# Reordering the setup of a four-layer graph-attention kernel: mask rows, first loads, and which step's work goes first

## The chip, the cores and the metric

The kernel runs on one NeuronCore of one Trainium2 chip. The metric is the device time of one execution in microseconds (us), the median of several executions. Before the change it is 2712.34 us (three runs, 2709.53 to 2713.56).

Six instruction streams appear in the profile: PE (TensorE matmul) with its weight loads PEld, DVE (VectorE), ACT (ScalarE), POOL (GpSimd) and SP (SyncE). A name with a q (ACTq, SPq) is the instruction queue of that engine; a DMA is issued there, and while an issue waits or is still being written out, nothing behind it in that queue starts.

## The reference, cut to what matters

Sixteen graphs of 1024 nodes with 256 features share one 1024 x 1024 integer adjacency matrix. Four attention layers follow one another:

```python
h = jnp.maximum(_layernorm(x, axis=-1), 0.0)
x = x + _L0_gnn_ref(h, adj, L0_gnn_W, L0_gnn_a)      # layers 1, 2, 3 likewise
# one layer, H heads of D features (H = 4, 1, 4, 1)
q = (h @ W).reshape(B, N, H, D)
e = e_src[:, :, None, :] + e_dst[:, None, :, :]      # q . a_src and q . a_dst, an N x N matrix per head
e = jnp.where(e >= 0, e, ALPHA * e)
e = jnp.where(mask, e, NEG_INF)                      # adj > 0 in layers 0 and 1, adj != 0 in 2 and 3
attn = jax.nn.softmax(e, axis=2)
out = elu(attn @ q)                                  # relu in layer 3
```

## The kernel before

A *step* is one layer of one graph; there are 64, and four graphs are in flight. For each step the kernel makes layer-norm statistics (`bn`), normalised rows (`xn`), their transposes (`hT`), projections (`whx`, `sd`) and a row `grow` that goes out to DRAM and comes back broadcast to all partitions (`gs`, copied into PSUM as `g`). Then, for each head, DVE makes eight tiles `w` (weights times mask) and PE multiplies them with `whx`. The masks are made once, from `adj`, transposed by PE. P = 128, C = 8, HALF = 4, K = 2.

```python
    def mask_block(jc):                       # one of 8 column blocks of adj
        def fetch_block():
            st["raw"] = work.tile([P, C, P], I32, name="w", bufs=WBUFS)
            nc.scalar.dma_start(out=st["raw"], in_=adj.rearrange("(c p) j -> p c j", p=P)[
                :, :, jc * P:(jc + 1) * P])                                       # L155
        def sign():
            nc.vector.tensor_scalar(st["sgn"][:, 0], st["raw"], -1.0, 1.0, ...)   # L160
        def turn():
            pm = st["pm"] = ps_acc.tile([P, C, P], BF16, name="acc")
            for c in range(C):
                nc.tensor.transpose(pm[:, c, :], st["sgn"][:, 0, c, :], identb)   # L166
        def mask():
            nc.vector.tensor_scalar(masks[0][:, jc, :], pm, 0.0, None, op0=ALU.is_gt)  # L170
            nc.scalar.activation(masks[1][:, jc, :], pm, AF.Square)                    # L171

    # preparation(n), 20 pieces: stats(0), stats(1), normalise(0), normalise(1),
    #   then per half: transpose k = 0, 1 (L221, L222) and four project(c) (L233 to L244),
    #   then factors (L251 to L255), rows (L260 to L264), fetch_heads (L278)
    #   stats:     8 bn_stats on DVE (L191), then 10 small POOL operations (L198 to L207)
    #   normalise: 4 ACT operations (L213)
    # weight_columns(l): vectors (DMA of a, L114), columns (8 DVE operations and sq, L124 to L131),
    #   bound (PE L137, DVE top L140, four POOL operations L141 to L144)
    # broadcast: g <- gs on ACT (L284);  weights: w on DVE (L289);  aggregate: PE L305, ACT L309
    ...
        load(0)                               # x of graph 0, SP queue (L177)
        load_weights(0)                       # SP queue (L103)
        layer[0][0]()                         # the vectors a of layer 0, SP queue
        for jc in range(C):
            blocks[jc][0]()                   # eight loads of adj, ACT queue
        load(1)
        ...                                   # preparation of step 0, mixed with the masks
        done["prepared"] = 1
        plan(1)
        planned = 2
        prepare(-2)                           # step 1: statistics to the first four projections
        emit_tiles(C, must=True)              # step 0: first two g, first eight w
        prepare(-1)                           # step 1: the rest
        for i in range(1, STREAMS):
            load_weights(i)
            if i > 1:
                load(i)
        for l, at in ((1, 1), (2, 8 * 3 + 5), (3, 8 * 5 + 5)):
            for i, piece in enumerate(layer[l]):
                later[at + i] = piece         # run after group `at + i`, eight groups a step
```

Of the kernel before, what the change touches and what calls it, by code (L numbers as in the profile page):

```python
# [23 lines left out]
F32 = mybir.dt.float32  # L24
BF16 = mybir.dt.bfloat16
I32 = mybir.dt.int32
U8 = mybir.dt.uint8
AF = mybir.ActivationFunctionType
ALU = mybir.AluOpType
# [3 lines left out]
P = 128  # L33
EPS = 1e-5
SHIFT = 60.0
STREAMS = 4
WBUFS = 18
# [20 lines left out]
def kernel(ctx: ExitStack, tc: tile.TileContext, x, adj, ws, avs, out):  # L58
    nc = tc.nc
    B, N, F = x.shape  # L60
    C = N // P
    K = F // P
    HALF = C // 2

    const = ctx.enter_context(tc.tile_pool(name="const", bufs=1))
# [3 lines left out]
    neghalf = const.tile([P, C], F32, name="neghalf")  # L69
    nc.gpsimd.memset(neghalf, -0.5)  # L70
    half1 = const.tile([P, 1], F32, name="half1")
# [3 lines left out]
    identb = const.tile([P, P], BF16, name="identb")  # L75

    masks = [const.tile([P, C, N], U8, name=f"mask{i}") for i in range(2)]
    wx = []
# [5 lines left out]
    cbias = [const.tile([P, 1], F32, name=f"cbias{l}") for l in range(len(LAYERS))]  # L84
    shift60 = const.tile([P, 1], F32, name="shift60")
    nc.gpsimd.memset(shift60, SHIFT)

    xpool = ctx.enter_context(tc.tile_pool(name="xpool", bufs=STREAMS))
    prep = ctx.enter_context(tc.tile_pool(name="prep", bufs=2))
    small = ctx.enter_context(tc.tile_pool(name="small", bufs=4))  # L90
    work = ctx.enter_context(tc.tile_pool(name="work", bufs=2))
# [7 lines left out]
    xs = {}  # L99
    state = [dict() for _ in steps]  # L100

    def load_weights(l):
        nc.sync.dma_start(out=wx[l][:, :, 0:F], in_=ws[l].rearrange("(k p) f -> p k f", p=P))  # L103

    def weight_columns(l):

        H, slope, hs, _ = LAYERS[l]
        D = F // H
        st = {}

        def vectors():
            st["a"] = prep.tile([P, HALF, H, D], F32, name="e")
            for part in range(2):
                nc.sync.dma_start(  # L114
                    out=st["a"][:, part],
                    in_=bass.AP(tensor=avs[l].tensor, offset=avs[l].offset + part * D,
                                ap=[[0, P], [hs, H], [1, D]]),
                )

        def columns():  # L120
            for k in range(K):
                for part in range(2):
                    prod = st["a"][:, 2 + part]
                    nc.vector.tensor_mul(  # L124
                        prod, wx[l][:, k, 0:F].rearrange("p (h d) -> p h d", h=H),
                        st["a"][:, part])
                    nc.vector.tensor_reduce(
                        wx[l][:, k, F + part * H:F + (part + 1) * H], prod, AX.X, ALU.add)
            st["sq"] = small.tile([P, K, H], F32, name="sq", bufs=1)
            wd = wx[l][:, :, F + H:F + 2 * H]  # L130
            nc.vector.tensor_tensor(st["sq"], wd, wd, op=ALU.mult)  # L131

        def bound():

            pn = ps_p.tile([P, H], F32, name="pp")
            for k in range(K):
                nc.tensor.matmul(pn, lhsT=ones, rhs=st["sq"][:, k, :], start=(k == 0),  # L137
                                 stop=(k == K - 1))
            top = small.tile([P, 1], F32, name="top", bufs=1)
            nc.vector.tensor_reduce(top, pn, AX.X, ALU.max)  # L140
            nc.gpsimd.tensor_tensor(top, top, half1, op=ALU.pow)  # L141
            nc.gpsimd.tensor_scalar(cbias[l], top, 16.01, None, op0=ALU.mult)
            nc.gpsimd.tensor_scalar(nbias[l], top, -16.01 * slope, None, op0=ALU.mult)
            nc.gpsimd.tensor_scalar(rbias[l], top, -16.01 * (1.0 - slope), SHIFT,  # L144
                                    op0=ALU.mult, op1=ALU.add)

        return vectors, columns, bound

    def mask_block(jc):

        st = {}

        def fetch_block():
            st["raw"] = work.tile([P, C, P], I32, name="w", bufs=WBUFS)
            nc.scalar.dma_start(out=st["raw"], in_=adj.rearrange("(c p) j -> p c j", p=P)[  # L155
                :, :, jc * P:(jc + 1) * P])

        def sign():
            st["sgn"] = work.tile([P, 2, C, P], BF16, name="w", bufs=WBUFS)
            nc.vector.tensor_scalar(st["sgn"][:, 0], st["raw"], -1.0, 1.0, op0=ALU.max,  # L160
                                    op1=ALU.min)

        def turn():
            pm = st["pm"] = ps_acc.tile([P, C, P], BF16, name="acc")
            for c in range(C):
                nc.tensor.transpose(pm[:, c, :], st["sgn"][:, 0, c, :], identb)  # L166

        def mask():
            pm = st["pm"].rearrange("p c i -> p (c i)")
            nc.vector.tensor_scalar(masks[0][:, jc, :], pm, 0.0, None, op0=ALU.is_gt)  # L170
            nc.scalar.activation(masks[1][:, jc, :], pm, AF.Square)  # L171

        return fetch_block, sign, turn, mask

    def load(b):
        xs[b] = xpool.tile([P, C, F], F32, name="x")
        nc.sync.dma_start(out=xs[b], in_=x[b].rearrange("(c p) f -> p c f", p=P))  # L177

    def preparation(n):

        b, l = steps[n]
# [4 lines left out]
        def stats(half):  # L186
            if half == 0:
                st["bn"] = small.tile([P, C, 6], F32, name="bn")
            bn = st["bn"]
            for c in range(half * HALF, (half + 1) * HALF):  # L190
                nc.vector.bn_stats(bn[:, c, :], xs[b][:, c, :])  # L191
            if half == 1:

                m0, s0, m1, s1 = (bn[:, :, i] for i in (1, 2, 4, 5))
                rstd = st["rstd"] = small.tile([P, C], F32, name="rstd")
                shift = st["shift"] = small.tile([P, C], F32, name="shift")
                dev = small.tile([P, C], F32, name="dev")
                nc.gpsimd.tensor_tensor(dev, m0, m1, op=ALU.subtract)  # L198
                nc.gpsimd.tensor_tensor(dev, dev, dev, op=ALU.mult)
                nc.gpsimd.tensor_scalar(dev, dev, 0.25, EPS, op0=ALU.mult, op1=ALU.add)  # L200
                nc.gpsimd.tensor_tensor(rstd, s0, s1, op=ALU.add)
                nc.gpsimd.tensor_scalar(rstd, rstd, 1.0 / F, None, op0=ALU.mult)
                nc.gpsimd.tensor_tensor(rstd, rstd, dev, op=ALU.add)
                nc.gpsimd.tensor_tensor(rstd, rstd, neghalf, op=ALU.pow)  # L204
                nc.gpsimd.tensor_tensor(shift, m0, m1, op=ALU.add)
                nc.gpsimd.tensor_tensor(shift, shift, rstd, op=ALU.mult)
                nc.gpsimd.tensor_scalar(shift, shift, -0.5, None, op0=ALU.mult)  # L207

        def normalise(half):
            xn = st["xn", half] = prep.tile([P, HALF, F], F32, name="xn")  # L210
# [165 lines left out]
    def prepare(upto):  # L376

        while agenda and agenda[0][0] <= upto:
            _, n, piece, last = agenda.pop(0)
            piece()  # L380
            if last:
                done["prepared"] = n + 1
# [53 lines left out]
    ending = []  # L436
    later = {}
    with tc.manual_schedule():
        blocks = [mask_block(jc) for jc in range(C)]
        layer = [weight_columns(l) for l in range(L)]  # L440
        load(0)
        load_weights(0)
        layer[0][0]()
        for jc in range(C):
            blocks[jc][0]()
        load(1)
        nc.vector.tensor_copy(identb, ident)
        first = [piece for _, piece in preparation(0)]
        first[0]()
        first[1]()  # L450
        layer[0][1]()
        layer[0][2]()
        first[2]()
        first[3]()
        for jc in range(3):
            for piece in blocks[jc][1:]:
                piece()

        for i, jc in ((4, 3), (6, 4), (10, 5), (12, None), (14, None)):
            if jc is not None:  # L460
                blocks[jc][1]()
            first[i]()
            first[i + 1]()
            if i == 6:
                first[8]()
                first[9]()
            if jc is not None:
                blocks[jc][2]()
                blocks[jc][3]()
        for piece in first[16:]:  # L470
            piece()
        for jc in range(6, C):
            for piece in blocks[jc][1:]:
                piece()
        done["prepared"] = 1
        plan(1)
        planned = 2
        prepare(-2)
        emit_tiles(C, must=True)
        prepare(-1)  # L480
        for i in range(1, STREAMS):
            load_weights(i)
            if i > 1:
                load(i)

        for l, at in ((1, 1), (2, 8 * 3 + 5), (3, 8 * 5 + 5)):
            for i, piece in enumerate(layer[l]):
                later[at + i] = piece
        for n in range(len(steps)):
            for k, (h, i0, per) in enumerate(groups(n)):  # L490
# [52 lines left out]
```

## Time and profile before

| | |
|---|---|
| span of the profiled execution | 2711.9 us |
| PE busy | 2567.2 us, 95% |
| DVE busy | 1900.3 us, 70% |
| ACT busy | 1229.6 us, 45% |
| POOL busy | 992.3 us, 37% |
| PE busy in the first 121 us | 58.22 us |
| first `w` tile on DVE | 78.25 us after the start |
| transfers, mean of the span | 48 GB/s |

The span is one program on one core, so a wait anywhere shows up in the time only if PE, or whatever PE waits for, is held by it. Three views are used. The chain of waits goes back from the last instruction, at each step to what released it. The timeline has start, duration, engine, line, operation, output and input, the count of merged instructions, and in square brackets the idle time ahead and what ended it. The table by stages gives the busy time of every engine in a stretch.

### The profile page before, as it was taken

The page shows a single profiled execution, that of the slowest core. Times are in us where ns is not written, and L with a number is a line of the kernel's source. Part 1 is how long each engine was busy: PE and PEld are TensorE (multiplying, and loading weights), DVE is VectorE, ACT ScalarE, POOL GpSimd, SP SyncE. Part 2 cuts the span into 40 slices and gives each one's busy share as a digit, 9 for nine tenths or more (in the row PEclk, how much of TensorE's full clock was granted, in tenths as well). Part 3 has the DMA queues.
Part 4 walks back from the last instruction along what each step waited for, and adds up shares of the span by engine and source line. Part 5 has one row for each costly group of instructions (what it writes and reads, how often), then busy time and mean ns, then how long its engine had stood idle before and what let it go on. Part 6 is the DMA issues. An engine that isn't in the chain of part 4 may idle for free.

```text
span 2711.9 us, 89498 instructions
## 1 busy us (share of the span) xinstructions
PE 2567.2 (95%) x40080; PEld 2269.2 (84%) x40080; DVE 1900.3 (70%) x2041; ACT 1229.6 (45%) x3337; POOL 992.3 (37%) x1242
## 2 busy tenths in 40 slices
PE   3799999999999999999999999999999999999998
PEld 2688888888888888888888888888888888788876
DVE  3796686477875688666876778748687567678752
ACT  3344445444354554544444454544435444444431
POOL 2133424423424534344242353442332443443321
PEclk9899999999999999999999999999999999999999
DMA  3211011012122011002201211101212110011111
GB/s 117 87 42 45 10 45 41 19 62 66 41 72 71 27 49 41 18 33 72 73 33 49 72 33 42 41 25 57 67 39 72 59 45 18 33 41 42 33 33 55
DMA packets 70846, 130.12 MB, mean 48 GB/s; under 512 B 6208, under 2 KB 49984, under 8 KB 70464
## 3 DMA queue, kind: packets, MB, share of 16 engines
q1 hardware_dynamic: 62144, 120.21, 13.5%
q8 instruction: 316, 5.18, 0.8%
q10 hardware_dynamic: 8320, 4.19, 0.6%
q14 instruction: 66, 0.54, 0.1%
HBM read 106.95 MB, written 17.43 MB: 46 GB/s over the span
## 4 chain that ended last, share of the span: by engine, by line
PE 81%; DVE 8%; ACT 4%; issue 3%; POOL 2%; DMA 1%; ACTq 0%; DVEq 0%; SPq 0%; POOLq 0%
PE acc L305 61%; PE pp L233 16%; DVE w L289 6%; PE pp L221 4%; ACT xn L213 1%; DVE bn L191 1%; DMA w<-in_adj 1%; ACT whx L235 1%; ACT g L284 1%; POOL rstd L204 0%; ACT e L339 0%; POOL y L330 0%; ACT whx L239 0%; PE pp L260 0%; DMA x<-in_x 0%
## 5 line engine op out<-in xcount | busy, mean ns | idle before, releaser
L305 PE MATMUL acc<-whx,w 128*64 128x65 f32 x36864 | 1951.0, 242 | 42.0 <-DVE w L289 28.6
L305 PEld LDWEIGHTS acc<-whx,w 128*64 128x64 f32 x36864 | 1766.8, 145 | 225.2 <-issue 70.4
L289 DVE SCALAR_TENSOR_TENSOR w<-g,rcol,mask 128x1024 f32<-128x1024 f32 x1280 | 1544.1, 1273 | 458.3 <-ACT g L284 412.3
L309 ACT ACTIVATE y<-acc 128x260 f32<-128x260 f32 (+1 forms) x512 | 196.8, 384 | 1085.8 <-PE acc L305 1085.0
L233 PE MATMUL pp<-wx,hT 128*128 128x258 f32 (+1 forms) x2048 | 513.2, 394 | 9.0 <-ACT hT L222 7.6
L330 POOL TENSOR_TENSOR y<-y,r 128x1024 f32<-128x1024 f32 x128 | 242.5, 1899 | 594.9 <-DVE r L326 594.9
L233 PEld LDWEIGHTS pp<-wx,hT 128*128 128x128 f32 x2048 | 375.1, 191 | 79.6 <-ACT hT L222 9.9
L346 POOL TENSOR_TENSOR x<-x,e 128x1024 f32<-128x1024 f32 x96 | 226.7, 2366 | 278.0 <-DVE e L345 264.2
L244 POOL TENSOR_TENSOR whx<-whx 128x256 f32<-128x256 f32 x256 | 159.9, 630 | 444.9 <-ACT whx L242 443.5
L213 ACT ACTIVATE xn<-x,shift,rstd 128x256 f32<-128x256 f32 x512 | 264.1, 590 | 126.3 <-POOL shift L207 126.0
L345 DVE SCALAR_TENSOR_TENSOR e<-e,y 128x1024 f32<-128x1024 f32 x96 | 117.6, 1225 | 197.0 <-ACT e L339 197.0
L235 ACT ACTIVATE whx<-pp,nbias 128x4 f32<-128x4 f32 (+1 forms) x512 | 135.0, 264 | 163.1 <-PE pp L233 151.8
L221 PE MATMUL pp<-ident,xn 128*128 128x128 f32 x1024 | 158.0, 287 | 39.0 <-ACT xn L213 28.3
L191 DVE BATCH_NORM_STATS2 bn<-x 128x6 f32<-128x256 f32 x512 | 172.9, 407 | 16.9 <-DMA x<-in_x 14.2
L221 PEld LDWEIGHTS pp<-ident,xn 128*128 128x128 f32 x1024 | 117.3, 144 | 76.7 <-ACT xn L213 36.3
L284 ACT ACTIVATE g<-gs 128x1024 f32<-128x1024 f32 x160 | 162.3, 1018 | 5.3 <-DVE w L289 5.3
L222 ACT ACTIVATE hT<-pp 128x512 f32<-128x512 f32 x256 | 143.2, 592 | 18.5 <-PE pp L221 16.5
L198 POOL TENSOR_TENSOR dev<-bn 128x8 f32<-128x8 f32 x64 | 16.4, 256 | 290.7 <-DVE bn L191 290.7
L239 ACT ACTIVATE whx<-pp,whx 128x256 f32<-128x256 f32 x256 | 121.7, 475 | 0.0
L339 ACT ACTIVATE e<-e 128x1024 f32<-128x1024 f32 x96 | 100.8, 1050 | 33.1 <-POOL e L335 33.1
L204 POOL TENSOR_TENSOR rstd<-rstd,neghalf 128x8 f32<-128x8 f32 x64 | 106.7, 1668 | 5.0
L335 POOL TENSOR_SCALAR e<-y 128x1024 f32<-128x1024 f32 x96 | 100.0, 1042 | 8.5
(45 smaller groups left out, 553.8 us busy)
## 6 DMA issues: line engine op xcount, KB each, us to landing
gs<-grow SPq DMA_DIRECT2D x160, 512.0 KB
x<-in_x SPq DMA_DIRECT2D x16, 1024.0 KB
out<-x SPq DMA_DIRECT2D x32, 512.0 KB
w<-in_adj ACTq DMA_DIRECT2D x8, 512.0 KB
wx<-in_L_gnn_W SPq DMA_DIRECT2D x4, 256.0 KB
e<-in_L_gnn_a SPq DMA_DIRECT2D x8, 128.0 KB
grow<-gT SPq DMA_DIRECT2D x32, 16.0 KB
grow<-gT SPq DMA_DIRECT2D x32, 4.0 KB
```

Of the source, the lines that this page charges most:

```text
L191: nc.vector.bn_stats(bn[:, c, :], xs[b][:, c, :])
L213: nc.scalar.activation(xn[:, q, :], xs[b][:, c, :], AF.Identity, bias=st["shift"][:, c:c + 1], scale=st["rstd"][:, c:c + 1])
L221: nc.tensor.transpose(pt[:, q, :], st["xn", half][:, q, k * P:(k + 1) * P], ident)
L233: nc.tensor.matmul(pw, lhsT=st["hT", half][:, k, q * P:(q + 1) * P], rhs=wx[l][:, k, :], start=(k == 0), stop=(k == K - 1))
L235: nc.scalar.activation(whx[:, c, :, D], pw[:, F + H:F + 2 * H], AF.Exp, bias=nbias[l], scale=slope)
L244: nc.gpsimd.tensor_tensor(whx[:, c, :, 0:D], whx[:, c, :, 0:D], whx[:, c, :, D:D + 1].to_broadcast([P, H, D]), op=ALU.mult)
L284: nc.scalar.activation(g, state[n]["gs", h], AF.Copy)
L289: nc.vector.scalar_tensor_tensor(w, state[n]["g", h], state[n]["rcol"][:, jc, h:h + 1], masks[LAYERS[steps[n][1]][3]][:, jc, :], op0=ALU.m ...
L305: nc.tensor.matmul(acc[o % P:o % P + cols, q, :], lhsT=st["w", h, jc][:, o:o + cols], rhs=st["whx"][:, jc, h, :], start=(jc == 0), stop=(j ...
L309: nc.scalar.activation(st["y"][:, i0:i0 + per, h, :], acc, AF.Copy)
L330: nc.gpsimd.tensor_tensor(yh, yh, r[:, :, None].to_broadcast([P, HALF * H, D]), op=ALU.mult)
L346: nc.gpsimd.tensor_add(xh, xh, e)
```

## The change

It rearranges the setup, so that the first step's work is held up by less, and leaves the steps' arithmetic as it is. The mask matrices come out the same.

1. `adj` is loaded in eight row chunks, each a contiguous row of 4 KB per partition, on the SP queue behind x of graph 0; before, it was eight column blocks in pieces of 512 B on the ACT queue. Each chunk is transposed into a column strip of the masks.
2. x of graph 0 comes in two loads, and step 0's statistics are combined for each half on DVE (all but the power) instead of once on POOL. A one-element `Exp` on ACT stands ahead of the first real one.
3. The transposed chunks 0 to 3 lie in the PSUM buffers of `g`, two to a buffer, so the second mask (`Square` on ACT) can be made from them after step 0's row is out.
4. Step 0's first `g` and `w` stand ahead of step 1's preparation (all but its statistics) in the order of instructions.
5. The weights of layer 1 are loaded early; `columns` and `bound` of layers 1 to 3 move to other groups.

```diff
-    def load_weights(l):
-        nc.sync.dma_start(out=wx[l][:, :, 0:F], ...)
+    def load_weights(l, queue=nc.sync):
+        queue.dma_start(out=wx[l][:, :, 0:F], ...)
...
-    def mask_block(jc):
+    pairs = {}
+    def mask_rows(c):
-            nc.scalar.dma_start(out=st["raw"], in_=adj.rearrange("(c p) j -> p c j", p=P)[
-                :, :, jc * P:(jc + 1) * P])
+            st["raw"] = work.tile([P, N], I32, name="w", bufs=WBUFS)
+            nc.sync.dma_start(out=st["raw"], in_=adj[c * P:(c + 1) * P, :])
...
         def turn():
-            pm = st["pm"] = ps_acc.tile([P, C, P], BF16, name="acc")
+            if c < HALF:
+                if c % 2 == 0:
+                    pairs[c // 2] = ps_g.tile([P, 2, C, P], BF16, name="g")
+                pm = pairs[c // 2][:, c % 2]
+            else:
+                pm = ps_acc.tile([P, C, P], BF16, name="acc")
...
-        def mask():
+        def positive():
+            nc.vector.tensor_scalar(masks[0][:, :, c * P:(c + 1) * P], st["pm"], 0.0, None,
+                                    op0=ALU.is_gt)
+        def nonzero():
+            nc.scalar.activation(masks[1][:, :, c * P:(c + 1) * P], st["pm"], AF.Square)
...
-            if half == 1:
-                ...                            # ten operations of 128 x 8 on POOL
+            if n == 0:
+                combine(slice(half * HALF, (half + 1) * HALF), nc.vector)
+            elif half == 1:
+                combine(slice(0, C), nc.gpsimd)    # the power is on POOL in both
...
-        load(0)
-        load_weights(0)
-        layer[0][0]()
-        for jc in range(C):
-            blocks[jc][0]()
+        load(0, 2)
+        layer[0][0](nc.scalar)
+        load_weights(0, nc.scalar)
+        for c in range(C):
+            blocks[c][0]()
         load(1)
+        load_weights(1)
+        nc.scalar.activation(warm, half1, AF.Exp)
...
+        # order of the second mask's chunks: 0, 4, 5, 6, 1, 2, 3, 7
+        first[0](); first[1](); first[2]()         # step 0: both halves' statistics, normalise(0)
+        layer[0][1]()                              # columns
+        first[3]()
+        sign_and_mask(False)                       # sign and turn of chunk 0
+        layer[0][2]()                              # bound
+        sign_and_mask()                            # sign and turn of the next, first mask of the last
+        for at in (4, 10):                         # one half each
+            first[at](); first[at + 1]()           # transposes
+            sign_and_mask()
+            first[at + 2](); first[at + 3]()       # two projections
+            sign_and_mask()
+            other_mask(1)
+            first[at + 4](); first[at + 5]()
+            sign_and_mask()
+            other_mask(1)
+        for piece in first[16:]:                   # row out, fetch
+            piece()
+        sign_and_mask()
+        other_mask(C)
...
-        prepare(-2)
+        for _ in range(2):                         # step 1: its statistics alone
+            agenda.pop(0)[2]()
         emit_tiles(C, must=True)
         prepare(-1)
-        for i in range(1, STREAMS):
+        for i in range(2, STREAMS):
             load_weights(i)
-            if i > 1:
-                load(i)
-        for l, at in ((1, 1), (2, 8 * 3 + 5), (3, 8 * 5 + 5)):
-            for i, piece in enumerate(layer[l]):
+            load(i)
+        for l, at in ((1, 1), (2, 8 * 3 + 3), (3, 8 * 5 + 3)):
+            for i, piece in zip((0, 1, 7), layer[l]):
                 later[at + i] = piece
```

More of the change, by code (lines that the diff above doesn't have):

```diff
@@ L86 @@
     nc.gpsimd.memset(shift60, SHIFT)
+    warm = const.tile([P, 1], F32, name="warm")
     xpool = ctx.enter_context(tc.tile_pool(name="xpool", bufs=STREAMS))
@@ L100 @@
     state = [dict() for _ in steps]
-    def load_weights(l):
-        nc.sync.dma_start(out=wx[l][:, :, 0:F], in_=ws[l].rearrange("(k p) f -> p k f", p=P))
+    def load_weights(l, queue=nc.sync):
+        queue.dma_start(out=wx[l][:, :, 0:F], in_=ws[l].rearrange("(k p) f -> p k f", p=P))
     def weight_columns(l):
@@ L109, in weight_columns, with vectors @@
         st = {}
-        def vectors():
+        def vectors(queue=nc.sync):
             st["a"] = prep.tile([P, HALF, H, D], F32, name="e")
             for part in range(2):
-                nc.sync.dma_start(
+                queue.dma_start(
                     out=st["a"][:, part],
@@ L147, in weight_columns, with fetch_rows @@
         return vectors, columns, bound
-    def mask_block(jc):
+    pairs = {}
+    def mask_rows(c):
         st = {}
-        def fetch_block():
-            st["raw"] = work.tile([P, C, P], I32, name="w", bufs=WBUFS)
-            nc.scalar.dma_start(out=st["raw"], in_=adj.rearrange("(c p) j -> p c j", p=P)[
-                :, :, jc * P:(jc + 1) * P])
+        def fetch_rows():
+            st["raw"] = work.tile([P, N], I32, name="w", bufs=WBUFS)
+            nc.sync.dma_start(out=st["raw"], in_=adj[c * P:(c + 1) * P, :])
         def sign():
-            st["sgn"] = work.tile([P, 2, C, P], BF16, name="w", bufs=WBUFS)
+            st["sgn"] = work.tile([P, 2, N], BF16, name="w", bufs=WBUFS)
             nc.vector.tensor_scalar(st["sgn"][:, 0], st["raw"], -1.0, 1.0, op0=ALU.max,
@@ L163, in turn, with load @@
         def turn():
-            pm = st["pm"] = ps_acc.tile([P, C, P], BF16, name="acc")
-            for c in range(C):
-                nc.tensor.transpose(pm[:, c, :], st["sgn"][:, 0, c, :], identb)
-        def mask():
[L169 to L175, printed above, removed]
+            if c < HALF:
[4 more added lines that the diff above has]
+                pm = ps_acc.tile([P, C, P], BF16, name="acc")
+            st["pm"] = pm
+            for jc in range(C):
+                nc.tensor.transpose(pm[:, jc, :], st["sgn"][:, 0, jc * P:(jc + 1) * P], identb)
+        def positive():
[3 more added lines that the diff above has]
+            nc.scalar.activation(masks[1][:, :, c * P:(c + 1) * P], st["pm"], AF.Square)
+        return fetch_rows, sign, turn, positive, nonzero
+    def load(b, parts=1):
         xs[b] = xpool.tile([P, C, F], F32, name="x")
-        nc.sync.dma_start(out=xs[b], in_=x[b].rearrange("(c p) f -> p c f", p=P))
+        xb = x[b].rearrange("(c p) f -> p c f", p=P)
+        for i in range(parts):
+            q = slice(i * C // parts, (i + 1) * C // parts)
+            nc.sync.dma_start(out=xs[b][:, q], in_=xb[:, q])
     def preparation(n):
@@ L191, in stats @@
                 nc.vector.bn_stats(bn[:, c, :], xs[b][:, c, :])
-            if half == 1:
[L194 to L207, printed above, removed]
+            if n == 0:
+                combine(slice(half * HALF, (half + 1) * HALF), nc.vector)
+            elif half == 1:
+                combine(slice(0, C), nc.gpsimd)
@@ new lines, in combine @@
+        def combine(q, engine):
+            bn = st["bn"]
+            m0, s0, m1, s1 = (bn[:, q, i] for i in (1, 2, 4, 5))
+            if q.start == 0:
+                st["rstd"] = small.tile([P, C], F32, name="rstd")
+                st["shift"] = small.tile([P, C], F32, name="shift")
+                st["dev"] = small.tile([P, C], F32, name="dev")
+            rstd, shift, dev = (st[i][:, q] for i in ("rstd", "shift", "dev"))
+            engine.tensor_tensor(dev, m0, m1, op=ALU.subtract)
+            engine.tensor_tensor(dev, dev, dev, op=ALU.mult)
+            engine.tensor_scalar(dev, dev, 0.25, EPS, op0=ALU.mult, op1=ALU.add)
+            engine.tensor_tensor(rstd, s0, s1, op=ALU.add)
+            engine.tensor_scalar(rstd, rstd, 1.0 / F, None, op0=ALU.mult)
+            engine.tensor_tensor(rstd, rstd, dev, op=ALU.add)
+            nc.gpsimd.tensor_tensor(rstd, rstd, neghalf[:, q], op=ALU.pow)
+            engine.tensor_tensor(shift, m0, m1, op=ALU.add)
+            engine.tensor_tensor(shift, shift, rstd, op=ALU.mult)
+            engine.tensor_scalar(shift, shift, -0.5, None, op0=ALU.mult)
@@ L438 @@
     with tc.manual_schedule():
-        blocks = [mask_block(jc) for jc in range(C)]
+        blocks = [mask_rows(c) for c in range(C)]
         layer = [weight_columns(l) for l in range(L)]
-        load(0)
-        load_weights(0)
-        layer[0][0]()
-        for jc in range(C):
-            blocks[jc][0]()
+        load(0, 2)
[3 more added lines that the diff above has]
+            blocks[c][0]()
         load(1)
+        load_weights(1)
@@ L447, with sign_and_mask @@
+        nc.scalar.activation(warm, half1, AF.Exp)
         nc.vector.tensor_copy(identb, ident)
         first = [piece for _, piece in preparation(0)]
+        turned, signed, masked = iter(range(C)), iter(range(C)), iter((0, 4, 5, 6, 1, 2, 3, 7))
+        def sign_and_mask(second=True):
+            c = next(signed, None)
+            if c is not None:
+                blocks[c][1]()
+                blocks[c][2]()
+            if second:
+                c = next(turned, None)
+                if c is not None:
+                    blocks[c][3]()
@@ L449, with other_mask @@
+        def other_mask(count):
+            for _ in range(count):
+                c = next(masked, None)
+                if c is not None:
+                    blocks[c][4]()
         first[0]()
         first[1]()
+        first[2]()
         layer[0][1]()
+        first[3]()
+        sign_and_mask(False)
         layer[0][2]()
[L453 to L469, printed above, removed]
+        sign_and_mask()
@@ L470 @@
+        for at in (4, 10):
+            first[at]()
+            first[at + 1]()
+            sign_and_mask()
+            first[at + 2]()
+            first[at + 3]()
+            sign_and_mask()
+            other_mask(1)
+            first[at + 4]()
+            first[at + 5]()
+            sign_and_mask()
+            other_mask(1)
         for piece in first[16:]:
             piece()
-        for jc in range(6, C):
-            for piece in blocks[jc][1:]:
-                piece()
+        sign_and_mask()
```

## The prediction, made before the changed kernel ran

> **What bounds the kernel now.** The busy shares come first: PE is busy 95% of 2711.9 us, DVE 70%. So the long middle belongs to PE, and a change of the setup can only win what PE loses before it is fed. The table by stages says how much that is (columns: stretch, length, then busy us and instruction count of PE, PEld, DVE, ACT, POOL, then granted clock, DMA share, GB/s):
>
> ```profile
> 0.00:121.00 121.00, 58.22 (x718) 46.69 (x718) 58.12 (x84) 43.10 (x107) 23.07 (x60) 0.86 0.36 109
> 121.00:600.00 479.00, 459.74 (x7645) 408.25 (x7647) 350.04 (x383) 221.50 (x600) 186.49 (x230) 0.98 0.12 38
> ```
>
> In the first 121 us PE idles 121 - 58.2 = 63 us; in the next 479 us only 19. The most the setup could give back is thus some 60 us, 2.3% of the time, and that with no setup at all. What holds PE is read from the chain of waits, from its start (start, length, what):
>
> ```profile
> 0.72 0.48 ACTq L155
> 1.20 0.03 issue
> 1.23 20.92 DMA w<-in_adj
> 22.14 0.02 issue
> 22.16 2.33 ACTq L155
> 24.50 0.04 issue
> 24.54 3.44 ACTq L155
> ...
> 29.56 1.28 ACT L213
> 30.84 0.01 issue
> 30.86 4.04 ACT xn L213 x8
> ```
>
> ACT, which must normalise the first rows, is still issuing loads of `adj` (L155) until 29.5 us, then loads its table, and starts `xn` at 30.86, though `shift` was there at 14.82 us (POOL L207, 14.58 + 0.24). Next the timeline, from step 0's row to its use:
>
> ```profile
> 54.43 0.27 ACT L262 ACTIVATE gT<-pp 32x128 f32<-32x128 f32 x1 [0.38 <-PE pp L260]
> ...
> 65.58 4.04 ACT L213 ACTIVATE xn<-x,shift,rstd 128x256 f32<-128x256 f32 x8 [5.88 <-POOL shift L207]
> ...
> 77.17 1.99 ACT L284 ACTIVATE g<-gs 128x1024 f32<-128x1024 f32 x2
> ...
> 78.25 9.62 DVE L289 SCALAR_TENSOR_TENSOR w<-g,rcol,mask 128x1024 f32<-128x1024 f32 x8 [16.98 <-ACT g L284]
> ```
>
> The row is ready at 54.70, and the table by stages shows the two broadcasts moving from 56 to 62 us and then nothing. Yet `g` is made at 77.17, because ACT does step 1's preparation first, and DVE waits 16.98 us for it. Then one more link, which decides what the gain is worth:
>
> ```profile
> 85.75 0.66 SPq L264 DMA_DIRECT2D grow<-gT  x1
> 86.46 0.94 SPq L103 DMA_DIRECT2D wx<-in_L_gnn_W  x2
> 87.45 0.47 SPq L177 DMA_DIRECT2D x<-in_x  x1
> ...
> 96.01 2.71 DVE L191 BATCH_NORM_STATS2 bn<-x 128x6 f32<-128x256 f32 x8 [8.14 <-DMA x<-in_x]
> ...
> 98.64 14.38 DVE L289 SCALAR_TENSOR_TENSOR w<-g,rcol,mask 128x1024 f32<-128x1024 f32 x12
> ```
>
> The second head's `w` stand on DVE behind the statistics of step 2, whose x is loaded behind step 1's row on the SP queue. So the steady state begins when x of graph 2 lands, at 96.0, and that hangs on the end of **step 1's** `gT` at 85.72. From 98.6 on DVE does not pause until after 200 us, and PE follows it. The shift of 96.0 is the gain.
>
> **What the Trainium skill says.** "DMA: Bandwidth & Descriptors", the section on the anatomy of one DMA, says that a wait for a semaphore is served by the issuing engine's sequencer before dispatch, not by the DMA engines: an issue that waits blocks what stands behind it. The trace agrees: 28.82 us of ACT's queue for eight issues. "ScalarE: Activation LUTs", what ACT_TABLE_LOAD costs: some 1283 ns; the trace has 1.28 us at 29.56. "TensorE: Matmul & The Clock Gate", part 1: PE runs at half rate until some 3.4 us of sustained work, and falls back after an idle window. The trace agrees: granted clock 0.50 from 60 to 70 us, and eight bf16 transposes (L166) take 1.04 us early, 0.61 later.
>
> **The change, part by part.** I follow the new order of instructions with durations of the old trace.
>
> *Loads.* The first x (1 MB) came by 7.76; half of it should be there at about 5.3, the rest by 7.5 (my reading of 231 to 346 GB/s between 2 and 8 us). The `adj` chunks follow at about 300 GB/s, the rate of the broadcasts in 4 KB rows (291 GB/s at 58 to 60 us): 0.52 MB each, 1.75 us, the first at 9.5, the last at 22. ACT issues three loads, some 0.5 us each, and its table is loaded by 4 us.
>
> *Statistics.* Four `bn` take 1.4 (8 take 2.71). Nine small DVE operations at about 0.23 (0.17 for `sq`, plus the hand-over) are 2.1, and the power between 0.96 (128x1) and 1.67 (128x8), say 1.3, with 0.15 of handing over. Half 0: 5.3 + 1.4 + 2.1 + 1.4 = 10.2, less 0.25 for the sum done meanwhile: 9.9. Half 1: 14.6. `xn` at 0.5 each: done at 12 and 16.7. That is 18 us ahead of the old 34.9, but not all of it stays.
>
> *Masks.* DVE makes the columns (8 operations at 0.42 and `sq`, 3.5) to 18.1, sign 0 (0.68) to 18.8, then waits for `bound` behind eight cold transposes: 2.1, to 20.9. From 21 on, PE, DVE and ACT alternate. PE: seven turns (1.04 cold for two, 0.62 after), 16 fp32 transposes (1.92 cold, 1.1 warm) and eight projections (1.03 each, 2.4 for the cold pair): 5.2 + 3.0 + 8.6 = 16.8. DVE: seven signs at 0.68 and seven masks at 1.23: 13.4, below PE's. Some 2 us for hand-overs, of which the tile-wide waits of the paired chunks and `hT` on ACT are the largest, give the last projection at 39 to 40. The Squares 1, 2, 3 and 7 come after the row. `rcol` to `gT` take 1.74 from 52.95 (the last `whx` done) in the old trace. So **row 0 ends at about 41.7, against 54.70: 13 us earlier.** The other 5 of the 18 us went to the masks, which now stand in the way instead of the loads.
>
> *Row to g.* Old: row at 54.70, transfers over by 61.6, 6.9 later for both; the first one about 5.7. New: first `g` at 47.4, second done at 49.6. The four Squares (4.1) and step 1's `bn` (2.7) fit under the transfer. First `w` at 48.5 against 78.25, but those eight are not what the end hangs on.
>
> *Step 1's preparation.* Old: `xn` at 65.58 to `gT` at 85.72, 20.14, with two `g` (1.99) inside; without them 18.2, the PE as cold as before. New: 49.6 + 18.2 = 67.8. So **step 1's row is 17.9 earlier**: 13 from part one, and about 5 because ACT no longer waits from 59.7 to 65.58 for POOL's chain, which now runs under the masks and the transfer.
>
> *x of graph 2.* Old: 85.72 to 96.0, 10.3. One weight load of 0.26 MB fewer ahead of it, at 284 to 298 GB/s 0.9, gives 9.4: 77.2. **The stream of `w` begins 18.8 earlier.**
>
> *Columns and bound later.* PE waited 4.4 us for layer 2's bound:
>
> ```profile
> PE pp L137 <- DVE sq L131: 4.4, 1, 4.4
> ```
>
> The bound now comes three groups later, but its 3.4 us of columns stand ahead of the next `bn` on DVE (257.45 us), where before they stood behind it, and `bn` feeds `xn`, which PE needs next (`xn` began at 264.97 and PE's transposes at 268.0). `xn` at 268.4 instead makes PE lose about 2 where it gained 1 by `bound` moved. For layer 3 the columns fall into DVE's 12.30 us of idling ahead of 347.33, where before they delayed the next `w`: 2 us of PE waits (0.43 + 0.92 + 0.70) go. Together between +1 and -2 us: I take 0.5 of gain.
>
> Sum: 18.8 + 0.5 = 19.3. 2712.3 - 19.3 = **2693 us**.
>
> **Rivals.** *(a) The new wait is as long as the old*: masks in the same stretch as the projections, with one more DVE wait at `bound`. For it: 16.8 us of PE against 13.4 of DVE, close enough that hand-overs could add 5; if the row ends at 47, the gain is 14 and the time 2699. *(b) Only the first eight `w` come early, and x of graph 2 eats it all.* For it: x is still behind step 1's row, and DVE would then idle from about 58 to 77. Against: that row itself moves by 18. If step 1 were held up by its own x (after all of `adj`, at about 25 us; needed at 40) it would fail, but 15 us of room are there. *(c) All 29.75 us by which the first `w` moves come through*: would need the second head free of x; the order on DVE speaks against it. Time then 2682. *(d) Small loads of `a` (256 B pieces) slow the first x*, since they now share the start with it: in the old trace `a` landed only at 14.0 and 21.9, beside the 512 B blocks. Two to four us lost if so: 2696.
>
> **Range and chances.** An error of 3 in the row, 1.5 in x, 2 in the columns and 2 in the runs make about 4.5 together; the range of 8 in 10 is 2685 to 2702. Faster by over 2% would need 54 us of the 63 that exist: 0.01. Slower by over 2% would need a new wait in every step, and none is added: 0.01.
>
> **What would show it.** `xn` of step 0 at 10 and 15 us, `gT` of step 0 at 42, first `w` at 48.5, `gT` of step 1 at 68, `bn` of step 2 waiting for x until 77, about 20 us of idling on DVE ahead of it, and the same stages afterwards. I am wrong if x of graph 2 comes off the row, if the masks hold the row past 47, or if stages after 121 us change by more than 3.

## The result, and the profile after

The changed kernel takes 2697.47 us (median of four executions, 2696.88 to 2702.25) against 2712.92 for the kernel before beside it. The ratio is 0.9949, with a 95% interval of 0.9932 to 0.9967: 15.4 us, 0.5%. The time lies inside the range; about four fifths of the expected 19.3 came.

The table by stages of the changed kernel, in the columns used before:

```profile
0.00:121.00 121.00, 68.16 (x1031) 57.15 (x1033) 74.79 (x115) 49.43 (x126) 23.97 (x56) 0.87 0.34 114
```

PE does 10 us more in the first 121 us (68.2 against 58.2). The chain of waits of the changed kernel, at its start:

```profile
0.72 0.48 ACTq L115
1.20 0.03 issue
1.23 0.59 ACTq L115
1.82 0.03 issue
1.85 20.20 DMA wx<-in_L_gnn_W
22.05 0.03 issue
22.08 0.02 DVEq L125
22.10 0.04 issue
22.14 0.44 DVE e L125
```

The loads of `adj` on ACT are gone from it. In their place stands a load of 0.26 MB, layer 0's weights, issued behind the two small vectors `a` (L115) and in flight for 20 us. The timeline shows the same start:

```profile
8.12 1.41 DVE L205 BATCH_NORM_STATS2 bn<-x 128x6 f32<-128x256 f32 x4 [6.40 <-DMA x<-in_x]
...
14.25 1.41 DVE L205 BATCH_NORM_STATS2 bn<-x 128x6 f32<-128x256 f32 x4 [2.06 <-DMA x<-in_x]
...
22.14 0.43 DVE L125 TENSOR_TENSOR e<-wx,e 128x256 f32<-128x256 f32 x1 [3.93 <-DMA wx<-in_L_gnn_W]
...
47.17 0.27 ACT L284 ACTIVATE gT<-pp 32x128 f32<-32x128 f32 x1 [0.38 <-PE pp L282]
...
54.73 9.63 DVE L311 SCALAR_TENSOR_TENSOR w<-g,rcol,mask 128x1024 f32<-128x1024 f32 x8 [5.93 <-ACT g L306]
```

x of graph 0 is late (8.12 and 14.25 us for its halves), the columns start at 22.14, the first row ends at 47.44. Further on:

```profile
73.81 0.27 ACT L284 ACTIVATE gT<-pp 32x128 f32<-32x128 f32 x1 [0.38 <-PE pp L282]
...
75.31 0.46 SPq L191 DMA_DIRECT2D x<-in_x  x1
...
81.66 2.71 DVE L205 BATCH_NORM_STATS2 bn<-x 128x6 f32<-128x256 f32 x8 [17.30 <-DMA x<-in_x]
```

DVE makes its first eight `w` and then idles 17.30 us for x of graph 2. The second batch of `w` starts at 84.29 instead of 98.64: 14.35 earlier.

### The profile page after: what moved, and what is told of

Read it like the earlier page. It is cut to its first block, busy times and chain, and to the rows that moved or that the text cites. A ratio compares the mean times of both kernels' runs of the same rounds, so it can differ in the third digit from the quotient of the medians.

```text
span 2700.4 us, 89532 instructions
## 1 busy us (share of the span) xinstructions
PE 2567.4 (95%) x40080; PEld 2271.1 (84%) x40080; DVE 1903.4 (70%) x2059; ACT 1228.1 (45%) x3338; POOL 987.8 (37%) x1234
## 4 chain that ended last, share of the span: by engine, by line
PE 82%; DVE 8%; ACT 4%; issue 3%; POOL 2%; DMA 1%; DVEq 0%; SPq 0%; ACTq 0%; POOLq 0%
PE acc L327 61%; PE pp L255 17%; DVE w L311 6%; PE pp L243 4%; DVE bn L205 1%; ACT xn L235 1%; DMA wx<-in_L_gnn_W 1%; POOL rstd L226 1%; ACT whx L257 1%; ACT g L306 0%; ACT e L361 0%; ACT whx L261 0%; PE pp L282 0%; ACT y L331 0%; POOL y L352 0%
## 5 line engine op out<-in xcount | busy, mean ns | idle before, releaser
L226 POOL TENSOR_TENSOR rstd<-rstd,neghalf 128x8 f32<-128x8 f32 (+1 forms) x65 | 107.0, 1646 | 19.2 <-DVE shift L227 14.3
```

## The experiments

Each kernel was timed beside the kernel before on the same chip. Because chips differ by a few us, times are given with that of the kernel before, and kernels timed on different chips are compared by their ratios to it. The new loads, the order and the groups of `columns` and `bound` are varied below. The statistics in two halves on DVE, the early `Exp` and the masks in the buffers of `g` were not undone on their own; what each of them brings isn't known.

### The changed kernel again

> The changed kernel once more, for a second trace and as the reference of the runs beside it. If the 4.5 us between its profiled execution (2702.3) and the other three (2697) are a matter of which PE idle times let the clock fall, the setup up to 84 us is the same in the second trace within 1 us, and the stages in which PE waits some 3 us for xn (near 167 us) differ. If they come from the first transfers, x of graph 0 lands at another time than 8.1 and 14.2 us. Expected: 2697.

Measured: 2699.43 against 2713.83, ratio 0.9946 (0.9934 to 0.9959). The setup is nearly the same: the first row ends at 47.53 instead of 47.44. The halves of x land within 1.2 us of where they did. The profiled execution was 2.8 us shorter in its span; 1.5 of that is one place, though not the one I named. The timeline of PE in the first trace and then in the second, at the same instructions:

```profile
433.86 4.63 PE L327 MATMUL acc<-whx,w 128*64 128x65 f32 x100 [0.85 <-DVE w L311]
```

```profile
433.66 3.14 PE L327 MATMUL acc<-whx,w 128*64 128x65 f32 x100 [0.86 <-DVE w L311]
```

The same hundred products take 4.63 us in one and 3.14 in the other, with a granted clock of 0.83 and 1.00 from 430 to 440 us. The waits ahead of them are the same. "TensorE: Matmul & The Clock Gate", part 1, says that the window over which activity is judged runs freely; two executions of one kernel with equal waits and unequal clocks agree with that. Differences of 2 us between single traces are therefore not read as effects below.

### Small loads behind x

```diff
-        layer[0][0](nc.scalar)
-        load_weights(0, nc.scalar)
+        layer[0][0]()
+        load_weights(0)
```

> The changed kernel, but with the vectors a and the weights of layer 0 on the SP queue behind x of graph 0 and ahead of adj, instead of on the ACT queue beside it. Theory A (the 256 B pieces of a, interleaved with x, hold x up): the halves of x land near 5 and 7.5 us instead of 8.1 and 14.2, xn of step 0 starts near 9 and 14, the columns do not wait until 22.1 for the weights, and the first row ends near 42 instead of 47.4. The time falls by 5, to 2692. Theory B (x is held up by the rows of adj behind it on its own queue, or by the two-part load itself): x lands as before, and the time stays at 2697.

Measured: 2697.10 against 2713.83, ratio 0.9940 (0.9927 to 0.9952): 2.3 us under the changed kernel beside it, half of what theory A said, with intervals that overlap. The timeline:

```profile
4.65 1.40 DVE L205 BATCH_NORM_STATS2 bn<-x 128x6 f32<-128x256 f32 x4 [2.92 <-DMA x<-in_x]
8.62 1.40 DVE L205 BATCH_NORM_STATS2 bn<-x 128x6 f32<-128x256 f32 x4
20.86 0.43 DVE L125 TENSOR_TENSOR e<-wx,e 128x256 f32<-128x256 f32 x1 [8.28 <-DMA wx<-in_L_gnn_W]
```

Theory A is right about x: with the small loads behind it, its first half is there at 4.65, and its second half costs DVE no wait. It is wrong about the columns: they still wait, until 20.86 instead of 22.14, and the first row ends at 46.06, not 42. The small loads are slow even when x is out of their way. The table by stages shows the transfers (the last two columns: share of the 16 engines, GB/s):

```profile
4.00:6.00 2.00, 0.00 (x0) 0.00 (x0) 1.35 (x4) 0.00 (x0) 0.00 (x0) 1.00 0.77 261
6.00:8.00 2.00, 0.00 (x0) 0.00 (x0) 1.02 (x8) 0.00 (x0) 0.72 (x1) 1.00 0.06 17
8.00:10.00 2.00, 0.00 (x0) 0.00 (x0) 1.62 (x6) 1.20 (x3) 0.31 (x1) 1.00 0.14 37
```

The 1024 pieces of `a` are most of the 1104 packets under 512 B that move between 4.9 and 19.8 us. From 6 to 10 us, while they are on their way, the engines are busy for 6 to 14% and move 17 to 37 GB/s. That isn't contention for bandwidth: they wait for something.

### a fetched once, and a from four addresses

In layer 0 all heads share `a`, so the load reads the same 256 B for 128 partitions times four heads, 512 times, for each of its two parts. Two kernels separate the number of pieces from the number of reads of one address. The first fetches once per partition:

```diff
+            copies = 1 if hs == 0 else H
...
-                    out=st["a"][:, part],
+                    out=st["a"][:, part, 0:copies],
...
-                        st["a"][:, part])
+                        st["a"][:, part] if hs or H == 1 else
+                        st["a"][:, part, 0:1].to_broadcast([P, H, D]))
```

The second keeps all 1024 pieces, but reads layer 2's vectors, where four heads lie at four addresses. Layer 0 then has other data:

```diff
+            src, step = (2, LAYERS[2][2]) if l == 0 else (l, hs)
...
-                    in_=bass.AP(tensor=avs[l].tensor, offset=avs[l].offset + part * D,
-                                ap=[[0, P], [hs, H], [1, D]]),
+                    in_=bass.AP(tensor=avs[src].tensor, offset=avs[src].offset + part * D,
+                                ap=[[0, P], [step, H], [1, D]]),
```

> As the run with the small loads behind x, but layer 0's vector a is fetched once per partition (256 pieces of 256 B) and broadcast over the four heads in the multiplication, instead of fetched four times (1024 pieces). The values are the same. Theory A (the pieces of a are slow one by one, about 80 to 90 per us, so their number counts): a and the weights of layer 0 land near 11 instead of 20.8, the columns start near 14.6, the first row ends near 41 to 42 and the time falls by 4 to 5 against the small loads behind x. Theory B (a is slow because it shares the engines with adj): a lands near 20 again, no gain.

> As the run with the small loads behind x, with 1024 pieces of 256 B again, but layer 0 reads its a from layer 2's vectors, whose four heads lie at four addresses, instead of 512 times the same 256 B. This changes the data of layer 0, the work is the same. Theory A1 (many reads of one address hold each other up): a lands near 10 to 12, as with one fetch per partition. Theory A2 (256 B pieces are slow whatever their address, their number counts): a lands near 20 again, and the time is that of the small loads behind x, 2697.

Measured: once per partition 2687.20 against 2712.51, ratio 0.9907 (0.9893 to 0.9920); four addresses 2689.21, ratio 0.9916 (0.9902 to 0.9930). By the ratios the first is some 9 us under the small loads behind x, twice what theory A said, and its first row ends at 36.68. The columns start at 12.52 and 12.53 us, straight behind the statistics. The second, in the timeline and in the table by stages at the times shown above:

```profile
12.53 0.43 DVE L126 TENSOR_TENSOR e<-wx,e 128x256 f32<-128x256 f32 x1
```

```profile
6.00:8.00 2.00, 0.00 (x0) 0.00 (x0) 1.07 (x8) 0.00 (x0) 0.68 (x1) 1.00 0.79 235
8.00:10.00 2.00, 0.00 (x0) 0.00 (x0) 1.57 (x6) 1.15 (x3) 0.36 (x1) 1.00 1.02 409
```

With as many pieces of the same size, but 128 instead of 512 reads of each address, 235 and 409 GB/s instead of 17 and 37. So A2 falls: neither the size nor the number of the pieces by itself makes `a` slow. "DMA: Bandwidth & Descriptors", specifications, puts the smallest piece at full rate at 512 B; here 1024 pieces of 256 B cost the columns nothing once they were spread over eight addresses.

The traces show the pace, too. From 6 to 7 us, 83 packets under 512 B move in the run with the small loads behind x (two addresses), 121 with one fetch per partition (two addresses) and 425 with eight. Fetching once helps because there is a quarter to fetch, not because each piece is much faster. And in the kernel before, layer 2's own 1024 pieces, from eight addresses, move within 3.1 us in mid-run (1072 packets under 512 B from 255.9 to 259.0 us), where layer 0's take 14 (from 7.5 to 21.6). This fits A1: **reads of one address held each other up**, and the loads beside them.

One rival stays open. The run with eight addresses also reads another vector, so a slow place of layer 0's vector in memory isn't excluded; and layer 3's vectors in the kernel before, 256 pieces of 1 KB from two addresses, moved within 2 us (343.5 to 345.5). What is shown is that the 1024 reads of layer 0's two addresses are slow, and that a quarter of them are no hindrance.

### The old kernel with a fetched once

> The kernel before, with layer 0's vector a fetched once per partition and broadcast in the multiplication; nothing else changed. Theory A (the 512 reads of one address also held the old setup: a landed at 14 and 21.9 there, and the last adj loads on ACT waited for it): a lands near 11, ACT is free of its loads near 22 to 24 instead of 29.5, the first row ends 5 to 8 earlier, and the time falls by about 6, to 2706. Theory B (the 512 B pieces of adj alone hold ACT until 29.5): a lands early, ACT is free at 28 to 30 all the same, and the time stays at 2712.

The edit is the one above, made in the kernel before. Measured: 2704.40 against 2711.85, ratio 0.9974 (0.9961 to 0.9987), 7.4 us. ACT's queue in the timeline of the kernel before and then of this one:

```profile
0.72 28.82 ACTq L155 DMA_DIRECT2D w<-in_adj  x8
```

```profile
0.72 19.91 ACTq L157 DMA_DIRECT2D w<-in_adj  x8
...
45.11 0.27 ACT L264 ACTIVATE gT<-pp 32x128 f32<-32x128 f32 x1 [0.38 <-PE pp L262]
```

ACT is free at 20.6, earlier than A said, and the first row ends at 45.38 instead of 54.70. From step 1 to step 10 the first evictions (ACT's first copy of a step's sums out of PSUM, L309 in the kernel before) are 8.4 us earlier throughout. So part of what the old chain booked as `adj` on ACT was the slow `a`, on the other queue: the eight issues wait for earlier transfers, and these were held up. One small edit to the old kernel brings about half of what the whole change did.

### Rows of adj on ACT's queue

```diff
-            nc.sync.dma_start(out=st["raw"], in_=adj[c * P:(c + 1) * P, :])
+            nc.scalar.dma_start(out=st["raw"], in_=adj[c * P:(c + 1) * P, :])
```

> The changed kernel, but with the eight row loads of adj issued on the ACT queue, behind a and the weights, as the block loads were before. Theory A (with 4 KB rows the loads come fast, and columns and masks set the pace to the first row, so ACT has slack): ACT is held until about 25, xn of step 0 starts near 26.5 instead of 12.3, but the first transposes on PE stand behind the second turned chunk at 29 to 30 anyway; the row ends within 1.5 us of 47.4 and the time is 2699 to 2701. Theory B (holding ACT's queue is what cost the old kernel its time): the row ends 5 or more later, and the time is 2704 or above.

Measured: 2701.89 against 2712.51, ratio 0.9962 (0.9949 to 0.9976), against 0.9946 (0.9934 to 0.9959) for the changed kernel: by the ratios 4 us of the gain are lost, but the intervals overlap, and the spans of the two traces are 2.6 us apart (2700.2 and 2697.6). ACT is held until 26.9 and `xn` starts at 28.35 instead of 12.28, yet the row ends at 48.62, only 1.2 later, as theory A said; the time is just above its 2701. Holding ACT thus cost the row little as long as the columns started at 19 to 22 us. What makes the rest of the difference isn't settled, and whether ACT's queue would cost more with `a` fetched once no run shows.

### The order of step 0 and step 1

Undone in the changed kernel:

```diff
-        for _ in range(2):
-            agenda.pop(0)[2]()
+        prepare(-2)
         emit_tiles(C, must=True)
```

> The changed kernel, but with the first ten pieces of step 1's preparation ahead of step 0's first g and w again, as before the change; loads, masks and statistics stay new. Theory A (the end hangs on the row of step 1, and ACT has the same work in either order): xn of step 1 starts near 53, its row ends near 73 to 75 as in the changed kernel (74.1), the first w come 12 us later without being missed, and the time is the changed kernel's within 2: 2697. Theory B (the early w are where the gain comes from): the time goes back by 10 or more, to 2707 or above.

And made alone in the kernel before (the same lines the other way round):

> The kernel before, with one part of the change alone: step 0's first g and w stand ahead of step 1's preparation, of which only the statistics go first. Loads, masks and all else are old. Theory A (the end hangs on the row of step 1): the row of step 0 ends at 54.7 as before, the first w start near 61.5 instead of 78.25, but xn of step 1 still waits for POOL until 65.6 and its row ends near 83.8 instead of 85.7; the time falls by 2, to 2711. Theory B (the 17 us by which the first w come earlier are won): 2697.

Measured: undone 2700.75 against 2713.83, ratio 0.9951 (0.9938 to 0.9963), within the interval of the changed kernel's 0.9946. The first `w` start at 64.33 instead of 54.73, step 1's row ends at 71.81, and the time doesn't show the ten us. Alone 2709.51 against 2711.85, ratio 0.9993 (0.9984 to 1.0002). Its timeline:

```profile
61.69 9.62 DVE L289 SCALAR_TENSOR_TENSOR w<-g,rcol,mask 128x1024 f32<-128x1024 f32 x8 [0.48 <-ACT g L284]
...
83.09 0.27 ACT L262 ACTIVATE gT<-pp 32x128 f32<-32x128 f32 x1 [0.37 <-PE pp L260]
...
92.17 2.71 DVE L191 BATCH_NORM_STATS2 bn<-x 128x6 f32<-128x256 f32 x8 [20.86 <-DMA x<-in_x]
```

The first `w` come 16.6 us earlier, step 1's row 2.4 earlier, and the wait that this opens on DVE is 20.86 us long. Theory A holds in both: the order by itself turned one wait into another.

### x of graph 2 early

```diff
         load(1)
+        load(2)
         load_weights(1)
...
-            load(i)
+            if i > 2:
+                load(i)
```

> The changed kernel, but with x of graph 2 loaded in the setup behind x of graph 1, instead of behind the row of step 1. Theory A (DVE's second batch of w hangs on that x alone): the 17.3 us wait of the statistics goes, the second batch starts near 67 instead of 84.3, PE aggregates without a break once the preparation of step 1 is done (about 74), and the time falls by 10 to 14, to about 2685. Theory B (the preparation of step 1 on ACT and PE sets the start of the steady state anyway, and w only wait elsewhere): 2695 to 2697.

Measured: 2685.85 against 2713.83, ratio 0.9894 (0.9879 to 0.9909): 13.6 us under the changed kernel beside it, at the upper end of theory A. The timeline:

```profile
65.61 2.71 DVE L205 BATCH_NORM_STATS2 bn<-x 128x6 f32<-128x256 f32 x8
68.22 9.62 DVE L311 SCALAR_TENSOR_TENSOR w<-g,rcol,mask 128x1024 f32<-128x1024 f32 x8
```

The statistics follow the first `w` without a wait, the second batch starts at 68.22 instead of 84.29, and PE is busy 75.5 us of the first 121. The trace is that of the longest of the four executions (2691.43 us). Whether the new order of step 0 and step 1 pays once x of graph 2 is early no run shows: none has x early and the order undone.

### Columns and bound

```diff
-        for l, at in ((1, 1), (2, 8 * 3 + 3), (3, 8 * 5 + 3)):
-            for i, piece in zip((0, 1, 7), layer[l]):
-                later[at + i] = piece
+        # groups 1, 2, 3 / 29, 30, 31 / 45, 46, 47, as before the change
```

> The changed kernel, but with columns and bound of layers 1 to 3 at the groups they had before. Theory A (from the traces: the move costs about 2 us near the end of step 3, where the columns stand ahead of the statistics that PE's transposes hang on, and brings 3 to 6 at the end of step 5, where they fill an idle DVE): up to 240 us the trace is the changed kernel's; PE waits 4.4 for layer 2's bound but starts step 4 about 1.5 earlier; PE waits for w again at the end of step 5. Net 1 to 3 slower: 2701. Theory B (a later bound is simply better everywhere): slower by 5 or more.

Measured: 2697.07 against 2712.51, ratio 0.9946 (0.9934 to 0.9959), the changed kernel's own: no net effect, where A said 1 to 3 slower and B 5 or more. The waits of PE from 240 to 275 us, in the changed kernel:

```profile
PE pp L243 <- ACT xn L235: 5.7, 1, 5.7
```

and with the old groups:

```profile
PE pp L138 <- DVE sq L132: 4.3, 1, 4.3
```

The move swaps one wait for a slightly longer one. The old groups are 2.5 us better there (first eviction of step 2 to that of step 4, against the second trace of the changed kernel) and 5.0 worse between the first evictions of steps 5 and 6 (301.62 to 350.33, against 307.01 to 350.75); by step 8 the two are within 0.6.

### All that helped, joined

> The changed kernel with the three edits that helped or may help joined: small loads behind x on the SP queue, a fetched once, x of graph 2 loaded in the setup. If the two gains lie one behind the other (the first row 11 us earlier, and the second batch of w freed from x), the second batch of w starts near 58, PE starts aggregating near 63, and the time is 2674 to 2677. If they overlap (PE is then held by the preparation of step 1 or by the w themselves), 2680 or more.

> As the joined kernel, and layer 2's columns and bound at the groups they had before the change, layer 3's at the new ones. From the trace with both undone (layer 2 at the old groups: 2.5 to 3.5 us gained around step 4; layer 3 at the new: 5 us gained at the end of step 5, 1.6 of it lost again): 2 to 4 us faster than the joined kernel, 2671 to 2674. If the idle times only move: the same as the joined kernel.

The first joins small loads behind x, `a` fetched once, and x of graph 2 early. Measured: 2675.50 against 2711.85, ratio 0.9870 (0.9853 to 0.9886), 36 us under the kernel before and more than twice the gain of the change. The second also moves layer 2's columns back: 2675.54, ratio 0.9871 (0.9857 to 0.9884), the same, where 2 to 4 us less were expected from the traces. In the first the row of step 0 ends at 37.93, the second batch of `w` starts at 57.27, and the aggregation begins at 64.07. The two gains lie one behind the other: the ratios of the two single kernels give 0.9946 - (0.9946 - 0.9907) - (0.9946 - 0.9894) = 0.9855, which is within the interval of the 0.9870 that was measured.

## Why the prediction was right

The chain was the right one: the second batch of `w` comes 14.35 us earlier, close to the gain of 15.4, and that shift is the sum of four links. Row 0 ends 7.3 earlier; from there to step 1's `xn` it takes 8.4 us instead of 10.9; that preparation takes 18.2 instead of 20.1; and x of graph 2 follows 7.6 us behind step 1's row instead of 10.3. One link was badly mis-sized, row 0. The total lies in the range because the range was wide enough for that error, and a smaller one at x offset part of it.

- *Loads.* The term that was mis-sized. Expected: halves of x at 5.3 and 7.5 us, columns from 14.6. Measured: 8.12, 14.25 and 22.14. I had taken the slow `a` of the old trace for contention with the 512 B blocks, made it rival (d) and gave it two to four us. That the small loads would cost something was right. But most of the cost came by another way, 7.5 us at the columns, which wait for the weights behind `a`; and neither the 512 B blocks nor the size of the pieces was the cause. So (d)'s 2696 lies next to the measured 2697.47 partly by luck. With `a` fetched once and behind x, the first half of x is there at 4.69, the second costs no wait, and the columns start at 12.52, all earlier than I had said.
- *Statistics.* The sum for nine operations and the power was close: 8.12 to 12.28 is 4.2 from the first `bn` to `xn`, against 4.6.
- *Masks.* From the columns to the end of the row I had 27.1; it took 25.3 (22.14 to 47.44), and 24.2 with `a` fetched once. So the row was at 47.44, not 41.7: 7.3 earlier than before, not 13. Rival (a) named 47 as the sign of masks in the way; the number came, by another road.
- *Row to g, and step 1's preparation.* First `g` 6.2 after the row (5.7 expected), step 1's `xn` to the end of its row 18.23 (18.2 expected).
- *x of graph 2.* 81.66 less 74.08 is 7.6, where I had 9.4; what makes it 1.8 shorter isn't settled. The link itself is shown by the early load: 13.6 us.
- *The stream of w.* 14.35 earlier instead of 18.8: 5.7 lost at the row and 0.5 at `g`, less the 1.8 that x returned.
- *Columns and bound.* 0.5 expected, none measured. The cost near 268 us was as described (PE's wait for `xn` 5.66 us). The gain before step 6 was 5.8 rather than 2 in the two traces (first evictions of steps 5 and 6: 9.3 and 15.1 us ahead), and 1.9 of it was left at step 8 (3.4 in the second trace).
- *After 121 us.* I asked for the same stages within 3 us. By the first evictions the lead of 14.3 at step 1 was 11.4 at step 2, where PE met a 3.04 us wait for `xn` and the granted clock fell to 0.62 (166 to 172 us), and 11.5 at the end. That trace is the longest of the four executions; in the second trace the spans differ by 14.3.
- *Rivals.* (b) was wrong as a claim that x of graph 2 takes all, and right in its idling (17.3 us); (c) is excluded by the order made alone, which brings the first `w` 16.6 us forward and wins 2.3.

## What to carry to other kernels

When a chain books a long time on a transfer, look at what the transfer engines did in it: here they were busy for 6% at 17 GB/s, so they were waiting, and the cure was to read less often from the same two addresses; moving the slow loads to another queue and behind x won 2.3 us, reading less often some 9 more. A value that many partitions and heads share is worth reading once per partition and spreading on chip. Bringing work forward paid little here as long as the operation that stood next on the same engine lacked its data; ask which load that is before moving anything.

## What the runs showed of the hardware

Two transfers of 128 KB, in 1024 pieces of 256 B, held the columns until 20.86 us when each of two addresses was read 512 times, and were no hindrance at 12.53 us when each of eight was read 128 times. During the slow reads the core's other loads crawled too, on the other queue as well: beside them the halves of x landed at 8.12 and 14.25 us, ahead of them the first at 4.65 and the second without a wait at 8.62. Why such reads hold each other up, and whether the place of the vector has a part in it, no run shows. And one stretch of a hundred products took 3.14 or 4.63 us in two executions of the same kernel, with the same wait ahead of it and a granted clock of 1.00 or 0.83.
